# A fused graph-attention kernel: step 0's small transfers on another queue, and the last span's sums ended in two halves

## The chip, the cores and the metric

The kernel runs on one core of one Trainium2 chip. The metric is the device time of one execution in microseconds (us), and a comparison uses the median of several runs. The core has five engines that run their own instruction lists in order and meet through semaphores: TensorE (PE, matrix products, with its weight loads shown as PEld), VectorE (DVE), ScalarE (ACT), GpSimd (POOL) and SyncE (SP). Transfers between memory and the core's buffers are issued from the list of an engine, here SP's or ACT's, and run on 16 DMA engines. SP does nothing but issue transfers.

## What is computed

Two layers work on x (2708 x 256) and adj (2708 x 2708). Cut to what matters:

```python
# layer 0: two steps of row-normalised adjacency and of sparse attention
R = (adj + I) / row_sums
for n in range(2):
    A  = top_p(softmax((Xa @ W1.T @ W2.T) @ (Xa @ W3.T).T), 0.9)   # rows re-normalised
    Xf = R @ Xf
    Xa = A @ Xa
    Z += Xf @ U1[n].T + Xa @ U2[n].T
x = layernorm(x + layernorm(x + Z))
# layer 1: graph attention with 4 heads of 64
Wh = einsum('nd,hdo->nho', x, W)
e  = leaky_relu(s_i[:, None] + s_j[None, :], 0.2)     # s_i, s_j: Wh times the halves of a
h  = softmax(e where adj or diagonal, over j) applied to Wh
x  = layernorm(x + h.reshape(n, 256))
```

## The kernel before

The 2708 rows are 22 tiles: 16 of 128 rows and 6 of 110 (`rows`, `off`). Most work is float32.

**Layer 0, step 0** (about 95 to 470 us of the trace). For each tile t, `step` multiplies its attention weights with all 22 tiles of values. The weights e have to be turned first: `turned` makes transposes on PE (`tr`, L266) and a copy on ACT (`eT`, L271), one group of up to four tiles ahead of the products (`att`, L284). Between groups, `slot` advances other work by one piece: searches for the top-p threshold of later tiles (DVE, ACT, POOL), and what comes after a finished tile. That last is `after_attention0`: it turns the tile's result, projects it for the next step's scores after every second tile (`project`) and multiplies it with the second pair of U matrices (`terms2`). Both of the latter end in a small transfer:

- `project` copies half of the query rows into the partition range `there` of qT (L766) and then moves them to the other half of the partitions with a transfer (L767, 55 to 64 KB). `begun` is empty before step 0 starts and set from then on, so the seven transfers of the first projection are SP's and the twelve of step 0 are ACT's.
- `terms2` copies a product into the buffer cs (L1257; two of these buffers rotate), a second one into ba (L1258), and stores cs to memory as c (L1259, 110 to 128 KB, one for each of the 22 tiles). The stores are read back when layer 0 is finished, after 500 us.

Beside this runs `mixes`: for each of 11 pairs of tiles SP loads four blocks of adj (L677), POOL adds and subtracts them, and SP stores the sums (L683) for a fast matrix product of layer 0's other half, `walks`, which loads them back (L689) from the end of step 0 on.

**Layer 1.** Targets are worked on in three `spans` of 8, 8 and 6 tiles (1024, 1024 and 660 columns). For each span a loop takes the 22 source tiles in pairs. `weights` makes the four heads' unnormalised weights pt on DVE (L1602), into three sets of buffers; `values` multiplies them with the source's values (L1614), `denominators` with its column sums (L1624), each head or half head in a quarter of PE's columns. Products are summed in six PSUM banks `acc`, for two head pairs and the denominators, each in two column pieces `cuts`, 512 and the rest (148 in the last span). After the last pair the banks are copied to `val` (L1717) and `den` (L1725), the first piece by ACT, the second by DVE.

`settle` then finishes one target tile, in pieces that a loop advances in turn: three transposes on PE (L1532, L1533), a reciprocal on DVE (L1535), the scaled result `res`, the add of the residual xe on POOL (L1551), and in the last span the layer norm: statistics on DVE (L1558 to L1560), a power and a product on POOL (L1561, L1562), the normalised tile o on ACT (L1564; two buffers o rotate) and its store by SP (L1565). In the last span res is made on ACT, a head at a time (L1546), for even tiles, and on DVE, in one operation (L1541), for odd ones. Tiles of the first two spans are settled beside the next span's products; those of the last span after all products, from six homes in PSUM.

In layer 0 (from `query_weights` on) and layer 1 the order of PE, DVE, ACT and POOL is the order in which the program issues their instructions.

Of the kernel before, what the change touches and what calls it, by code (L numbers as in the profile page):

```python
# [12 lines left out]
ALU = mybir.AluOpType  # L13
# [7 lines left out]
CHUNK = 512  # L21
# [24 lines left out]
def kernel(  # L46
# [16 lines left out]
    nc = tc.nc  # L63
    N, D = x.shape
    DA = w1T.shape[1]
    STEPS = u1T.shape[0]
    H, _, FO = gat_w.shape
# [3 lines left out]
    rows = [P] * 16 + [110] * 6  # L71
# [31 lines left out]
    xe = const.tile([P, NT, D + 2], F32, name="xe")  # L103
# [448 lines left out]
    def fast_layer0(ep, adjp):  # L552
# [196 lines left out]
        def project(s, c0, w, pj, xT, copy_q, copy_k):  # L749

            for lo, hi, h in ((c0, min(c0 + w, HN), 0), (max(c0, HN), c0 + w, 1)):
                if lo >= hi:
                    continue
                here, there = slice(h * DA, (h + 1) * DA), slice((1 - h) * DA, (2 - h) * DA)
                at = slice(lo - c0, hi - c0)
                for c in range(DC):  # L760
                    nc.tensor.matmul(
                        pj[:, at], wkqk[:, c, h : h + 2].rearrange("p h e -> p (h e)"),
                        xT[:, c, at], start=(c == 0), stop=(c == DC - 1),
                    )
                copy_k(kT[s][here, lo - h * HN : hi - h * HN], pj[here, at])
                copy_q(qT[there, lo:hi], pj[there, at])  # L766
                (nc.scalar if begun else nc.sync).dma_start(qT[here, lo:hi], qT[there, lo:hi])  # L767

        def turn(src, m, tp, copy, xT=None):

# [476 lines left out]
        def terms2(t, xT):  # L1247

            m = rows[t]
            cy = free_bank().rearrange("p a b -> p (a b)")  # L1250
            for c in range(DC):
                nc.tensor.matmul(
                    cy[:m], xT[:, c, :m], u_sb[:, 1, c].rearrange("p s e -> p (s e)"),
                    start=(c == 0), stop=(c == DC - 1),
                )
            cs = rowp.tile([P, D], F32, name="cs")
            nc.scalar.copy(cs[:m], cy[:m, 0:D])  # L1257
            nc.scalar.copy(ba[:m, t, :], cy[:m, D : 2 * D])  # L1258
            nc.scalar.dma_start(c2[t][:m], cs[:m])  # L1259

        def finish(t, xw, ca, cb):

# [133 lines left out]
        with tc.manual_schedule(engines=engines):  # L1396
            query_weights()
            ahead = turn_x(groups[0])
            for n in range(len(groups)):
                c0, w = ahead  # L1400
# [95 lines left out]
    def layer1(ep, adjp, r=None, verdict=None, early=()):  # L1496
# [19 lines left out]
        def bank(k, c):  # L1516
            return ps_v[k][c].tile([P, CHUNK], F32, name=f"acc{k}_{c}")
# [6 lines left out]
        def aux():  # L1524
            return ps_u.tile([P, H, P], F32, name="aux")

        def settle(g, t, val, den, u, last):

            m = rows[t]
            cols = slice(off[t] - off[spans[g][0]], off[t + 1] - off[spans[g][0]])  # L1530
            for q in range(2):
                nc.tensor.transpose(u[:m, q, :], val[:, q, cols], ident)  # L1532
            nc.tensor.transpose(u[:m, 2, :], den[:, cols], ident)  # L1533
            rden = small.tile([P, H], F32, name="rden")
            nc.vector.reciprocal(  # L1535
                rden[:m], u[:m, 2, :].rearrange("p (h o) -> p h o", h=H)[:, :, 0]
            )
            res = pp.tile([P, H, FO], F32, name="res", bufs=5)
            sums = u[:m, 0:2, :].rearrange("p q (h o) -> p (q h) o", h=2)
            if last and t % 2:  # L1540
                nc.vector.tensor_tensor(  # L1541
                    res[:m], sums, rden[:m].unsqueeze(2).to_broadcast([m, H, FO]), op=ALU.mult
                )
            else:
                for h in range(H):
                    nc.scalar.activation(  # L1546
                        res[:m, h, :], sums[:, h, :], AF.Copy, scale=rden[:m, h : h + 1]
                    )
            yield
            flat = res[:m].rearrange("p h o -> p (h o)")  # L1550
            nc.gpsimd.tensor_add(flat, flat, xe[:m, t, 0:D])  # L1551
            yield
            o = pp.tile([P, D], F32, name="o")[:m]
            if last:
                st = small.tile([P, 6], F32, name="ln_st")[:m]
                mv = small.tile([P, 2], F32, name="ln_mv")[:m]
                ve, rs, nb = (small.tile([P, 1], F32, name=f"ln_{k}")[:m] for k in ("ve", "rs", "nb"))
                nc.vector.bn_stats(st, flat)  # L1558
                nc.vector.bn_aggr(mv, st)
                nc.vector.tensor_scalar(ve, mv[:, 1:2], LN_EPS, None, op0=ALU.add)  # L1560
                nc.gpsimd.tensor_tensor(rs, ve, minus_half[:m], op=ALU.pow)  # L1561
                nc.gpsimd.tensor_scalar(nb, mv[:, 0:1], rs, -1.0, op0=ALU.mult, op1=ALU.mult)  # L1562
                yield
                nc.scalar.activation(o, flat, AF.Identity, scale=rs, bias=nb)  # L1564
                nc.sync.dma_start(out[off[t] : off[t + 1], :], o)  # L1565
                return
            yield from layernorm_beside(o, flat, m)
            yield
            nc.scalar.dma_start(out[off[t] : off[t + 1], :], o)
# [10 lines left out]
        cuts = []  # L1580
        for span in spans:
            gw = off[span[-1] + 1] - off[span[0]]
            cuts.append([(c, min(CHUNK, gw - c)) for c in range(0, gw, CHUNK)])
        targets, masks, probs, acc = {0: r}, {}, {}, {}

        def mask(n):
# [17 lines left out]
                        bar, op0=ALU.max, op1=ALU.mult,  # L1604
                    )

        def values(n, heads):
            g, at, j = order[n]
            k, at = rows[j], dict(start=(at == 0), stop=(at == NT - 1), skip_group_check=True)
            for c, (c0, w) in enumerate(cuts[g]):  # L1610
                for h in heads:
                    for o in range(0, FO, SIDE):
                        to = h % 2 * FO + o
                        nc.tensor.matmul(  # L1614
                            acc[h // 2][c][to : to + SIDE, :w],
                            v[j][:k, h, o : o + SIDE], probs[n][h][:k, c0 : c0 + w], **at,
                        )

        def denominators(n):
            g, at, j = order[n]  # L1620
            k, at = rows[j], dict(start=(at == 0), stop=(at == NT - 1), skip_group_check=True)
            for c, (c0, w) in enumerate(cuts[g]):
                for h in range(H):
                    nc.tensor.matmul(  # L1624
                        acc[2][c][h * SIDE : (h + 1) * SIDE, :w],
                        sb[:k, j, h : h + 1].to_broadcast([k, SIDE]),
                        probs[n][h][:k, c0 : c0 + w], **at,
                    )
            del probs[n]

        def prepared(t):

# [64 lines left out]
        for n in range(0, len(order), 2):  # L1697
            g, i, j = order[n]
            beside(g, i)
            weights(n + 2)  # L1700
            mask(n + 3)
            if i == 0:
                acc = [
                    [bank(k, c) for c in range(len(cuts[g]))]
                    for k in range(3)
                ]
            last = i + 2 == NT
            if last:
                val = pp.tile([P, 2, GW], F32, name="val", bufs=1)
                den = pp.tile([P, GW], F32, name="den", bufs=1)  # L1710
            for u in (n, n + 1):
                for k in range(2):
                    values(u, (2 * k, 2 * k + 1))
                    if last and u > n:
                        for c, (c0, w) in enumerate(cuts[g]):
                            copy = nc.scalar.copy if c == 0 else nc.vector.tensor_copy
                            copy(val[:, k, c0 : c0 + w], acc[k][c][:, :w])  # L1717
            if not last:
                beside(g, i + 1)
            for u in (n, n + 1):  # L1720
                denominators(u)
            if last:
                for c, (c0, w) in enumerate(cuts[g]):
                    copy = nc.scalar.copy if c == 0 else nc.vector.tensor_copy
                    copy(den[:, c0 : c0 + w], acc[2][c][:, :w])  # L1725
                assert not rest
                rest = [(g, t, val, den) for t in spans[g]]
            weights(n + 3)
            mask(n + 4)
        assert not late  # L1730

        homes = [bank(k, c) for k in range(2) for c in range(2)]
        while rest or running:
            new = []
            if rest:
                u = homes.pop(0).rearrange("p (h m) -> p h m", h=H) if homes else aux()
                new = [settle(*rest.pop(0), u, True)]
                next(new[0])
            running = [p for p in running[::-1] if next(p, running) is not running][::-1] + new
        l1.close()  # L1740

    with ExitStack() as both:
# [58 lines left out]
```

## Time and profile before

| | us |
|---|---|
| median of 3 runs | 1546.16 |
| lowest and highest of them | 1543.17, 1548.04 |
| the profiled execution's own time | 1544.92 |
| its span in the trace | 1543.1 |
| mean granted clock of TensorE | 0.994 |

The page's slices (40 of 38.6 us each) show where the engines work, in tenths:

```profile
PE   7999999999999899999999999999999999999995
DVE  3698999888614887888889898998895998999995
ACT  3444445444426655665655666666653444456474
POOL 0057576654013422323354544544443320035133
DMA  6188988885027745544474565555446355334331
```

Step 0 covers slices 3 to 12. DMA is its busiest part: the mixing loads and stores run there, and end well before the step does. Layer 1 starts near 1200 us. The last slice is where PE has run out of products.

In the lists of groups and waits, `x` gives a count, `out<-in` the buffers written and read, and `<-` in brackets or after the wait what ended the idle time. ACTq and SPq are transfers issued from these engines' lists. ACT's largest waits of step 0's stretch:

```profile
ACT e L795 <- PE lg L791: 50.1, 20, 2.9
ACT cs L1257 <- PE walk L1252: 47.3, 19, 2.9
ACT eT L271 <- PE tr L266: 40.9, 34, 1.8
...
ACT eT L271 <- DMA scr<-in_adjT_dram: 11.8, 4, 5.7
ACT eT L271 <- ACT qT L766: 4.4, 8, 0.6
ACT eT L271 <- DMA D<-blk: 3.1, 2, 1.7
```

The columns are us in total, times, and the longest. The last three lines are idle time before an eT copy that was ended neither by PE nor by a search.

### The profile page before, as it was taken

The page shows a single profiled execution, that of the slowest core. Times are in us where ns is not written, and L with a number is a line of the kernel's source. Part 1 is how long each engine was busy: PE and PEld are TensorE (multiplying, and loading weights), DVE is VectorE, ACT ScalarE, POOL GpSimd, SP SyncE. Part 2 cuts the span into 40 slices and gives each one's busy share as a digit, 9 for nine tenths or more (in the row PEclk, how much of TensorE's full clock was granted, in tenths as well). Part 3 has the DMA queues.
Part 4 walks back from the last instruction along what each step waited for, and adds up shares of the span by engine and source line. Part 5 has one row for each costly group of instructions (what it writes and reads, how often), then busy time and mean ns, then how long its engine had stood idle before and what let it go on. Part 6 is the DMA issues. An engine that isn't in the chain of part 4 may idle for free. (4 is left out here: it accounts for less than half of the span.)

```text
span 1543.1 us, 29894 instructions
## 1 busy us (share of the span) xinstructions
PE 1494.1 (97%) x10537; PEld 1066.1 (69%) x10537; DVE 1275.3 (83%) x3741; ACT 807.7 (52%) x1494; POOL 590.6 (38%) x962
## 2 busy tenths in 40 slices
PE   7999999999999899999999999999999999999995
PEld 4476767677679888998888888888898223433343
DVE  3698999888614887888889898998895998999995
ACT  3444445444426655665655666666653444456474
POOL 0057576654013422323354544544443320035133
PEclk9999999999999999999999999999999999999998
DMA  6188988885027745544474565555446355334331
GB/s 167 63 251 280 283 273 255 267 263 168 8 77 223 228 160 169 166 151 147 146 210 126 176 193 160 187 168 176 130 146 185 104 179 170 97 107 131 87 111 46
DMA packets 214489, 255.98 MB, mean 166 GB/s; under 512 B 42145, under 2 KB 180541, under 8 KB 214329
## 3 DMA queue, kind: packets, MB, share of 16 engines
q1 hardware_dynamic: 201632, 243.15, 51.7%
q10 hardware_dynamic: 12697, 10.82, 2.3%
q8 instruction: 85, 1.39, 0.4%
q14 instruction: 75, 0.61, 0.1%
HBM read 190.10 MB, written 62.44 MB: 164 GB/s over the span
## 5 line engine op out<-in xcount | busy, mean ns | idle before, releaser
L816 ACT ACTIVATE junk<-e,minus,rth 128x2708 bf16<-128x2708 f32 (+1 forms) x88 | 232.9, 2646 | 52.5 <-POOL rth L848 51.7
L271 ACT COPY eT<-tr 128x512 f32<-128x512 f32 (+5 forms) x264 | 141.4, 536 | 213.4 <-PE tr L266 189.0
L284 PE MATMUL att<-xm,eT 128*128 128x256 f32 (+3 forms) x968 | 232.0, 381 | 0.4 <-ACT xa L1325 0.4
L284 PE MATMUL att<-ba,eT 128*128 128x256 f32 (+3 forms) x968 | 231.6, 380 | 0.0
L1614 PE MATMUL acc<-pt,v 128*32 128x512 f32 (+3 forms) x2112 | 221.0, 543 | 1.9 <-DVE pt L1602 1.2
L1602 DVE SCALAR_TENSOR_TENSOR pt<-e,tj,blk 128x1024 f32<-128x1024 f32 (+3 forms) x176 | 186.6, 1126 | 9.4 <-ACT xw L1265 6.5
L284 PEld LDWEIGHTS att<-xm,eT 128*128 128x128 f32 (+3 forms) x968 | 170.5, 187 | 22.4 <-ACT xa L1325 0.8
L284 PEld LDWEIGHTS att<-ba,eT 128*128 128x128 f32 (+3 forms) x968 | 170.1, 187 | 22.2 <-ACT eT L271 0.8
L795 ACT ACTIVATE e<-lg 128x1024 f32<-128x1024 f32 (+1 forms) x132 | 121.1, 922 | 106.6 <-PE lg L791 105.7
L1109 PE MATMUL walk<-xe,blk 128*128 128x128 f32 (+3 forms) x1386 | 172.9, 275 | 1.2 <-ACT xw L1123 0.7
L1109 PEld LDWEIGHTS walk<-xe,blk 128*128 128x128 f32 (+1 forms) x1386 | 164.4, 187 | 11.4 <-issue 7.4
L1614 PEld LDWEIGHTS acc<-pt,v 128*32 128x32 f32 (+1 forms) x2112 | 73.2, 110 | 132.3 <-issue 99.7
L266 PE MATMUL tr<-ident,e 128*128 128x128 f32 (+3 forms) x968 | 148.7, 272 | 12.1 <-ACT eT L271 11.9
L266 PEld LDWEIGHTS tr<-ident,e 128*128 128x128 f32 (+3 forms) x968 | 111.6, 139 | 55.9 <-issue 25.7
L1109 PE MATMUL walk<-xm,blk 128*128 128x128 f32 (+3 forms) x1034 | 130.4, 276 | 4.5 <-DVE u_sb L1119 2.7
L1109 PEld LDWEIGHTS walk<-xm,blk 128*128 128x128 f32 (+3 forms) x1034 | 123.3, 187 | 12.8 <-issue 6.1
L896 DVE MAX8 cand<-e 128x8 f32<-128x170 f32 (+1 forms) x352 | 88.0, 322 | 46.3 <-ACT e L795 46.3
L1624 PE MATMUL acc<-pt,sb 128*32 128x512 f32 (+3 forms) x1056 | 114.8, 542 | 0.0
L1602 DVE SCALAR_TENSOR_TENSOR pt<-r,tj,blk 128x1024 f32<-128x1024 f32 (+1 forms) x88 | 109.9, 1314 | 1.2 <-PE acc L1624 0.4
L247 ACT ACTIVATE blk<-blk 128x1024 f32<-128x1024 f32 (+3 forms) x66 | 63.2, 960 | 81.6 <-DMA blk<-in_adjT_dram 80.1
L896 DVE MAX8 cand<-scr 128x8 f32<-128x97 f32 (+1 forms) x616 | 102.9, 244 | 0.0
L802 POOL TENSOR_TENSOR fact<-zp 128x1 f32<-128x1 f32 (+1 forms) x44 | 30.0, 681 | 170.2 <-ACT e L795 170.2
(280 smaller groups left out, 2453.9 us busy)
## 6 DMA issues: line engine op xcount, KB each, us to landing
blk<-in_adjT_dram SPq DMA_DIRECT2D x68, 512.0 KB
blk<-S SPq DMA_DIRECT2D x48, 512.0 KB
blk<-D SPq DMA_DIRECT2D x24, 512.0 KB
blk<-in_adjT_dram SPq DMA_DIRECT2D x26, 440.0 KB
D<-blk SPq DMA_DIRECT2D x16, 512.0 KB
S<-scr SPq DMA_DIRECT2D x16, 512.0 KB
S<-blk SPq DMA_DIRECT2D x16, 512.0 KB
xm<-S SPq DMA_DIRECT2D x16, 512.0 KB
```

The lines of the kernel that those rows point to most:

```text
L247: nc.scalar.activation(bar, bar, AF.Sign)
L266: nc.tensor.transpose(tr[: rows[t], q, :m], e[:m, off[t] : off[t + 1]], ident[:m, :m])
L271: copy(eT[:k, : len(grp), :m], tr[:k, : len(grp), :m])
L284: nc.tensor.matmul(acc, eT[: rows[t], q, :m], value(t), start=(t == 0), stop=(t == NT - 1),)
L795: nc.scalar.activation(halves[:m, :, c0 : c0 + w], lg[:m, :, :w], AF.Exp, accum_out=zp[:m, n : n + 1],)
L802: nc.gpsimd.tensor_add(z, zp[:m, 0:1], zp[:m, 1:2])
L816: nc.scalar.activation(junk[:m], e[:m], func, scale=rth, bias=minus1[:m], accum_out=acc)
L896: nc.vector.max(cand[:, n, :], src[:m, n * size : min(N, (n + 1) * size)])
L1109: nc.tensor.matmul(ac, blk[:k, j, :], MOVING[name](j, k, w), start=start and j == 0, stop=j == PAIRS - 1, skip_group_check=True,)
L1602: nc.vector.scalar_tensor_tensor(pt[:k, :gw], targets[g][h // 2][:k, h % 2, :gw], tj[:k, j, h : h + 1], bar, op0=ALU.max, op1=ALU.mult,)
L1614: nc.tensor.matmul(acc[h // 2][c][to : to + SIDE, :w], v[j][:k, h, o : o + SIDE], probs[n][h][:k, c0 : c0 + w], **at,)
L1624: nc.tensor.matmul(acc[2][c][h * SIDE : (h + 1) * SIDE, :w], sb[:k, j, h : h + 1].to_broadcast([k, SIDE]), probs[n][h][:k, c0 : c0 + w], **at,
```

## The change

Four edits. The transfers of `project` and of `terms2` are always issued by SP. In the last span the column pieces are two halves of 330 columns, three tiles each. The last pair of sources of the last span goes through a new function, `closing`: it takes the first half's products of both sources, with their denominators, then the second half's of the first source, then starts to settle the three tiles of the first half, then takes the second half's products of the last source and settles the other three. Copies of the values are made by ACT for heads 0 and 1 and by DVE for heads 2 and 3, those of the denominators by ACT. And in `settle`, odd tiles of the last span get their residual in the same DVE operations that scale, one for each head, so that POOL's add falls away for them.

```diff
-                (nc.scalar if begun else nc.sync).dma_start(qT[here, lo:hi], qT[there, lo:hi])
+                nc.sync.dma_start(qT[here, lo:hi], qT[there, lo:hi])
...
-            nc.scalar.dma_start(c2[t][:m], cs[:m])
+            nc.sync.dma_start(c2[t][:m], cs[:m])
...
+            flat = res[:m].rearrange("p h o -> p (h o)")
             if last and t % 2:
-                nc.vector.tensor_tensor(
-                    res[:m], sums, rden[:m].unsqueeze(2).to_broadcast([m, H, FO]), op=ALU.mult
-                )
+                for h in range(H):
+                    nc.vector.scalar_tensor_tensor(
+                        res[:m, h, :], sums[:, h, :], rden[:m, h : h + 1],
+                        xe[:m, t, h * FO : (h + 1) * FO], op0=ALU.mult, op1=ALU.add,
+                    )
...
             yield
-            flat = res[:m].rearrange("p h o -> p (h o)")
-            nc.gpsimd.tensor_add(flat, flat, xe[:m, t, 0:D])
-            yield
+            if not (last and t % 2):
+                nc.gpsimd.tensor_add(flat, flat, xe[:m, t, 0:D])
+                yield
...
-            cuts.append([(c, min(CHUNK, gw - c)) for c in range(0, gw, CHUNK)])
+            part = CHUNK if span is not spans[-1] else len(span) // 2 * rows[span[0]]
+            cuts.append([(c, min(part, gw - c)) for c in range(0, gw, part)])
...
+        def begin(t, val, den, home):
+            new = settle(len(spans) - 1, t, val, den, home, True)
+            next(new)
+            step_on()
+            running.append(new)
+
+        def step_on():
+            running[:] = [p for p in running[::-1] if next(p, running) is not running][::-1]
+
+        def closing(n, val, den):
+
+            per = len(spans[-1]) // 2
+            early_ones, late_ones = spans[-1][:per], spans[-1][per:]
+            for c, (c0, w) in enumerate(cuts[-1]):
+                these = slice(c, c + 1)
+                for u in (n, n + 1):
+                    if c and u > n:
+                        for k, t in enumerate(early_ones):
+                            begin(t, val, den, bank(k, 0).rearrange("p (h m) -> p h m", h=H))
+                    for k, copy in enumerate((nc.scalar.copy, nc.vector.tensor_copy)):
+                        values(u, (2 * k, 2 * k + 1), these)
+                        if u > n:
+                            copy(val[:, k, c0 : c0 + w], acc[k][c][:, :w])
+                    denominators(u, these)
+                nc.scalar.copy(den[:, c0 : c0 + w], acc[2][c][:, :w])
+            for k, t in enumerate(late_ones):
+                home = aux() if k < 2 else bank(0, 1).rearrange("p (h m) -> p h m", h=H)
+                begin(t, val, den, home)
+            while running:
+                step_on()
...
+            if last and g == len(spans) - 1:
+                closing(n, val, den)
+                break
...
-        homes = [bank(k, c) for k in range(2) for c in range(2)]
-        while rest or running:
-            new = []
-            if rest:
-                u = homes.pop(0).rearrange("p (h m) -> p h m", h=H) if homes else aux()
-                new = [settle(*rest.pop(0), u, True)]
-                next(new[0])
-            running = [p for p in running[::-1] if next(p, running) is not running][::-1] + new
```

`values` and `denominators` take a third argument, the pieces to work on.

More of the change, by code (lines that the diff above doesn't have):

```diff
@@ L1605, in weights, with values @@
                     )
-        def values(n, heads):
+        def values(n, heads, these=None):
             g, at, j = order[n]
             k, at = rows[j], dict(start=(at == 0), stop=(at == NT - 1), skip_group_check=True)
-            for c, (c0, w) in enumerate(cuts[g]):
+            for c, (c0, w) in list(enumerate(cuts[g]))[these or slice(None)]:
                 for h in heads:
@@ L1617, in values, with denominators @@
                         )
-        def denominators(n):
+        def denominators(n, these=None):
             g, at, j = order[n]
             k, at = rows[j], dict(start=(at == 0), stop=(at == NT - 1), skip_group_check=True)
-            for c, (c0, w) in enumerate(cuts[g]):
+            for c, (c0, w) in list(enumerate(cuts[g]))[these or slice(None)]:
                 for h in range(H):
@@ L1628, in denominators @@
                     )
-            del probs[n]
+        def begin(t, val, den, home):
[25 more added lines that the diff above has]
+                step_on()
         def prepared(t):
@@ L1721, in layer1 @@
                 denominators(u)
+                del probs[u]
             if last:
```

## The prediction

> **What bounds the kernel now.** I read the page's busy line first, then the waits of TensorE, then the two places the change touches: layer 0's step 0 (95 to 470 us) and the tail after 1509 us.
>
> ```profile
> PE 1494.1 (97%) x10537; PEld 1066.1 (69%) x10537; DVE 1275.3 (83%) x3741; ACT 807.7 (52%) x1494; POOL 590.6 (38%) x962
> ```
>
> TensorE (PE) is busy 1494.1 of 1543.1 us, so a gain is a PE gap closed or something after PE's last product. For step 0, PE's own waits between 95 and 470 us, then ScalarE (ACT) in order of time around the longest of them and around a later one:
>
> ```profile
> PE tr L266 <- ACT eT L271: 5.5, 4, 3.3
> PE lg L774 <- ACT xa L1325: 0.6, 1, 0.6
> PE walk L761 <- ACT qT L766: 0.5, 1, 0.5
> ...
> 112.09 0.37 ACT L766 COPY qT<-walk 64x256 f32<-64x256 f32 x1
> 117.64 0.50 ACTq L767 DMA_DIRECT2D qT<-qT  x1
> 118.18 0.59 ACT L271 COPY eT<-tr 128x512 f32<-128x512 f32 x1 [5.72 <-DMA scr<-in_adjT_dram]
> ...
> 275.24 0.38 ACT L1258 COPY ba<-walk 128x256 f32<-128x256 f32 x1
> 277.53 0.33 ACTq L1259 DMA_DIRECT2D c<-cs  x1
> 277.90 0.59 ACT L271 COPY eT<-tr 128x512 f32<-128x512 f32 x1 [2.28 <-DMA scr<-in_adjT_dram]
> ```
>
> ACT finished qT's copy at 112.46 but issued the transfer after it only at 117.64; the copy of eT that PE needed stood behind it, and ACT's idle time ended with a landing of scr, a block that the transfer has nothing to do with. In the program's list of waits every transfer waits for an earlier one that used the same of eight completion semaphores, so a small store issued by ACT can wait for a 512 KB load that SyncE (SP) issued. PE's four gaps before L266 are 3.25 us (to 118.82), 0.35 (172.31), 0.49 (227.72) and 1.44 (278.54), together 5.53, and each follows such an issue on ACT.
>
> The first gap costs more than itself. Busy time by stretch (us of PE, PEld, DVE, ACT, POOL; clock; DMA share; GB/s):
>
> ```profile
> 115.20:118.60 3.40, 0.36 (x1) 0.00 (x0) 3.19 (x6) 0.42 (x1) 3.40 (x4) 1.00 0.97 319
> 118.60:122.00 3.40, 3.18 (x10) 2.73 (x11) 3.37 (x5) 1.30 (x4) 3.40 (x4) 0.50 0.99 382
> 122.00:125.40 3.40, 3.40 (x18) 2.50 (x18) 3.40 (x3) 0.37 (x1) 3.40 (x2) 1.00 0.80 304
> ```
>
> After an idle stretch PE runs 3.4 us at half clock: 1.7 us of work lost. In the tail, the chain of waits (start, us, what) shows PE's last products, and the timeline (start, us, engine, line) a result on DVE, the first adds on POOL and the last output tile:
>
> ```profile
> 1521.89 1.99 PE acc L1624 x18
> 1523.89 0.02 issue
> 1523.91 0.59 ACT den L1725
> ...
> 1525.52 0.42 DVE L1541 TENSOR_TENSOR res<-acc,rden 110x256 f32<-110x256 f32 x1
> ...
> 1526.13 1.31 POOL L1551 TENSOR_TENSOR res<-res,xe 110x256 f32<-110x256 f32 x2 [9.01 <-ACT res L1546]
> ...
> 1535.94 0.60 ACT L1564 ACTIVATE o<-res,ln_nb,ln_rs 110x256 f32<-110x256 f32 x1 [0.56 <-DMA out_dram<-o]
> ```
>
> Products end at 1523.89, the last o at 1536.54, the span at 1543.1. In the 12.65 us between, GpSimd (POOL) sets the pace: each of six tiles takes an add (0.64 to 0.72), a power (0.55) and a product (0.27) there, about 1.5 us.
>
> [...]
>
> **The change, part by part.**
>
> *A. Step 0's transfers go to SP.* Twelve qT transfers (L767) and 22 c stores (L1259) leave ACT's queue. Of PE's time: 5.53 us of gaps go, and 3.4 x 0.5 = 1.7 us of slow clock with the first. Sum 7.2. The issue time that ACT sheds (12 x 0.47 + 22 x 0.33 = 12.9 us) is worth nothing more, because ACT is 42% busy there (156.2 of 375 us) and other eT copies come in time. What is late next: VectorE's (DVE) searches, 93.1 of 100 us busy between 200 and 300. They are ahead, though: DVE's last reciprocal of step 0 ends at 420.29, and the last tile, whose result ACT copies at 449.71, starts some 18 us before that, near 431, so 7 us fits.
>
> On SP every issue counts. Thirty-four more take 12.9 us, and each waits for ACT's copy. I set each new place in SP's list against the times of before: at 24 of the 34, the SP transfer just behind it was issued 0.5 to 8.5 us after ACT's copy was done, at three the copy is 0.03 to 0.35 us later, and seven fall where SP idles until 449.28 anyway. Queued behind them are the mixing loads and stores (L677, L683). Those end at 366.2, and four block loads at 369; the next SP load then waits for PE until 449.28. That is the cover, 80 us, against 24 moved issues (about 9.5 us) before it. Only two stand after 449, with ACT's copies done at 455.26 and 460.06 and SP's next issues at 456.35 and 460.53: up to 0.5 us for a walk load, where PE has gaps on loads at 503.5 and 507.6 us. I take 0, bound 0 to 1. The stores land later by 5 to 10 us; their two cs buffers turn over every 15 us per tile, c is read after 500 us, qT's other half by the next step's rows. No wait there.
>
> *B. The tail.* I laid out the last pair of sources and the settling by hand, in the new order of each engine's list, with durations of before's rows; the same layout of the old order ends at 1536.43 (traced: 1536.54). One pair's 96 product records take 4.58 + 2.22 = 6.80 us. A half (330 columns) of one source is thus 1.70, of it 0.57 for denominators. A 330-column width costs the same per column as 512 and 148, so the rest of the span is priced at 0.
> - PE: start 1516.7; first source's first half to 1518.4. The last source's weights come from DVE at 1518.09, 1518.90, 1519.72, 1520.54 as before (they wait for a buffer that PE frees at 1516.7). So PE waits 0.5, works 0.57, waits 1.1, works 1.14: 1521.7. First source's second half: 1523.4. Nine transposes at 0.11: 1524.4. Last source's second half: 1526.1, 2.2 us later than before.
> - Early tiles: ACT's result of the first 1524.2 to 1525.1, POOL's add to 1525.9, its mean and variance on DVE to 1527.1. Behind this in DVE's list stands the second half's val copy: 1527.1 to 1527.55, while PE had that product at 1525.6.
> - Late tiles: transposes from 1527.6; DVE's four-operation results and statistics end 1530.0 (tile 19), 1530.8, 1532.7, 1533.5; POOL's last power and product 1533.7 to 1534.6; last o 1534.65 to 1535.24.
>
> Against 1536.43 that is 1.2 us earlier. Three adds (2.0 us) leave POOL, but DVE gains three sets of four. Not in the trace: a 64-column scalar_tensor_tensor from PSUM. Below, a quarter of the 256-column row at L1541 (0.425/4), so 0.12; above, the 56-column L955 at 0.28 to 0.335. [...] I take 0.20. Twelve of them: the gain runs from 1.9 (0.12) through 1.2 to a loss of 0.6 (0.35). The 6.6 us after the last o stay.
>
> Sum: 7.2 + 1.2 = 8.4. The profiled execution took 1544.92, which gives 1536.5; the median of the three is 1546.16, which gives 1537.8. I say 1537.
>
> **Rivals.**
> 1. *Half of A stays.* DVE at 93% becomes step 0's pace, or the half-clock stretch moves: a gap of 2.7 us at 807.7 is followed by one, a gap of 2.4 at 1189.6 is not[...]. Then only the 3.3 of the long gap and B's 1.2 come: 1541.7. For: DVE's share. Against: its lead at the end of the step.
> 2. *The tail gives B back.* DVE operations cost 0.35, the copy of val is later: B is +0.6, total 6.6 less, 1539.5. For: DVE has the most new work, and PE's products end later.
> 3. *SP holds the mixing (slower).* A store waiting for ACT holds all mixing transfers behind it, POOL waits for loads, ACT and PE come later in turn. Place: SP between 96 and 369 us; price: the hold of each of 24 moved issues; it decides once these average 80/24 = 3.3 us. At 4 us, 16 us late: 1546.2 - 8.4 + 16 = 1554. For: DMA is 88 to 90% busy from 100 to 300 us. Against: ACT's copies are ready ahead of SP nearly everywhere.
> 4. *It doesn't do what it says*: the gaps reappear on ACT for another transfer; B alone, 1545. Against: no transfer is left on ACT in step 0.
>
> **How the numbers follow.** Forecast 0.58, rival 1 0.17, rival 2 0.10, rival 3 0.09, rival 4 0.06. A measurement here tells 0.3% (4.6 us; faster is below 1541.5). Faster: 0.55 of the forecast, 0.09 of rival 2, 0.05 of rival 1, 0.69. Slower: rival 3, 0.09. The rest, 0.22, within. Range: low end 1537.8 less 1.7 (a second half-clock stretch gone), 0.7 (B at its best) and 2.9 (the lowest run against the median): 1532.5. High end past rival 1 with half of the runs' spread: 1544. That leaves out rivals 3 and 4.
>
> **What would show it.** Right: no waits of ACT's eT copy on DMA between 95 and 470 us, PE's wait there on eT under 1 us, no half clock near 118, step 0 ending near 442; SP's mixing done by 385. In the tail: products ending about 2.2 us later against the start of the last pair, DVE's second val copy 1.5 us after its product, last o about 18.6 us after that start (19.8 before). Wrong: new PE gaps in step 0 with releaser DVE or DMA, SP still issuing mixing stores after 430, or four DVE results per tile taking over 1.2 us.

## The result, and the profile after

| | before | after |
|---|---|---|
| median, us (5 runs of each) | 1544.79 | 1534.79 |
| lowest and highest, us | 1541.94, 1548.04 | 1533.26, 1537.31 |
| span of the profiled execution, us | 1543.1 | 1532.7 |

The ratio is 0.993, with a 95% interval of 0.9916 to 0.9944. The kernel is faster by 10.0 us; the prediction said 1537 us.

I read the profile after in the order in which the one before was read. First the page's busy line:

```profile
PE 1492.8 (97%) x10537; PEld 1064.6 (69%) x10537; DVE 1277.1 (83%) x3749; ACT 804.9 (53%) x1495; POOL 594.5 (39%) x959
```

PE's work is the same (10537 instructions) and takes 1.3 us less; the rest of the gain must be time in which PE idled. Then PE's waits between 95 and 470 us (line, what it waited for, us in total, times, longest), and ACT in order of time (start, us, what) where it had stood for 5.2 us:

```profile
PE lg L774 <- ACT xa L1325: 0.6, 1, 0.6
PE walk L761 <- ACT qT L766: 0.5, 1, 0.5
PE att L284 <- ACT xa L1325: 0.3, 2, 0.2
```

```profile
112.10 0.37 ACT L766 COPY qT<-walk 64x256 f32<-64x256 f32 x1
112.49 0.58 ACT L271 COPY eT<-tr 128x512 f32<-128x512 f32 x1
```

The first line of the old list, 5.5 us for eT, is gone. The copy of eT starts at 112.49, directly behind qT's copy, where it had started at 118.18. The end of step 0 is read here as the start of PE's transposes at L774 that follow the step's last att product: 450.24 us before, 441.91 after. The windows from 95 us to it in each kernel (length; busy PE, PEld, DVE, ACT, POOL; clock; DMA share; GB/s), before first, and then, in after, the same stretch of time that had run at half clock before:

```profile
95.00:450.24 355.24, 348.12 (x1740) 252.30 (x1739) 290.78 (x853) 150.91 (x336) 186.37 (x206) 1.00 0.68 211
```

```profile
95.00:441.91 346.91, 345.49 (x1741) 251.51 (x1739) 291.71 (x853) 148.32 (x336) 192.51 (x206) 1.00 0.70 216
118.60:122.00 3.40, 3.40 (x18) 1.76 (x17) 3.40 (x2) 1.16 (x3) 3.40 (x4) 1.00 1.00 398
```

Step 0 is 8.33 us shorter. PE's idle time in it fell from 7.12 (355.24 - 348.12) to 1.42 us, which is 5.70; its busy time fell by 2.63, of which 1.61 is the half-clock stretch, as worked out further down (the clock column now has 1.00 there).

In the tail, the chain of waits of after (start, us, what), and PE's last products and first transposes of the late tiles in its timeline:

```profile
1516.18 0.86 DVE res L1543 x4
1517.05 0.09 DVE rden L1535
1517.13 0.38 DVE ln_st L1561
1517.54 0.19 DVE ln_mv L1562
1517.76 0.15 DVE ln_ve L1563
1517.91 0.35 DVE ln_st L1561
...
1518.65 0.42 DVE val L1656
...
1526.08 0.60 ACT o L1567
```

```profile
1517.25 0.74 PE L1628 MATMUL acc<-pt,sb 110*32 110x330 f32 x8
1518.47 0.32 PE L1532 MATMUL aux<-ident,val 128*110 128x128 f32 x1 [0.48 <-ACT val L1656]
1519.12 0.32 PE L1532 MATMUL aux<-ident,val 128*110 128x128 f32 x1 [0.32 <-DVE val L1656]
```

The chain now runs through DVE, where before POOL set the pace. DVE works without a break from the first fused result to the second half's val copy, which waits behind the statistics of two early tiles; PE's transposes for the late tiles wait for it.

To compare tails of traces that are shifted against each other I use one mark: the start of DVE's last operation on the diagonal (L251), shortly before the last sources' weights, at 1516.81 us before and 1508.31 after. From there the last o ends after 19.73 us before and 18.37 after, 1.36 less. PE's products end after 7.31 and 9.68. The whole difference of the two spans, -10.45 us, is then:

| stretch | difference, us |
|---|---|
| step 0, to the first transposes of xa (L774) | -8.33 |
| from there to the start of the tail | -0.17 |
| tail, from the mark to the end of the last o | -1.36 |
| after the last o | -0.59 |

I put the two differences in rows 2 and 4 down to no edit: the time after the last o lies between 5.62 and 7.09 us over all traces of the study, and the largest parts of row 2 are a gap of PE at 1182 us that is shorter (1.29 against 2.44) and one at 1280 that is longer (1.81 against 0.49). Over all traces the first lies between 1.20 and 2.66 us and the second between 0.45 and 2.13, and after_again, the same kernel as after, has 1.49 and 0.50.

### The profile page after: what moved, and what is told of

Its sections match the earlier page's. It is cut to its first block, busy times and chain, and to the rows that moved or that the text cites. A ratio compares the mean times of both kernels' runs of the same rounds, so it can differ in the third digit from the quotient of the medians.

```text
span 1532.7 us, 29967 instructions
## 1 busy us (share of the span) xinstructions
PE 1492.8 (97%) x10537; PEld 1064.6 (69%) x10537; DVE 1277.1 (83%) x3749; ACT 804.9 (53%) x1495; POOL 594.5 (39%) x959
## 5 line engine op out<-in xcount | busy, mean ns | idle before, releaser
L1109 PE MATMUL walk<-xe,blk 128*128 128x128 f32 (+3 forms) x1386 | 172.9, 275 | 1.2 <-ACT xw L1123 0.7
L1109 PEld LDWEIGHTS walk<-xe,blk 128*128 128x128 f32 (+1 forms) x1386 | 164.4, 187 | 11.4 <-issue 7.4
L266 PE MATMUL tr<-ident,e 128*128 128x128 f32 (+3 forms) x968 | 147.5, 271 | 4.8 <-ACT eT L271 4.8
L266 PEld LDWEIGHTS tr<-ident,e 128*128 128x128 f32 (+3 forms) x968 | 111.3, 139 | 47.1 <-issue 26.7
L1109 PE MATMUL walk<-xm,blk 128*128 128x128 f32 (+3 forms) x1034 | 131.3, 277 | 5.4 <-DVE u_sb L1119 2.9
L1109 PEld LDWEIGHTS walk<-xm,blk 128*128 128x128 f32 (+3 forms) x1034 | 124.2, 188 | 14.0 <-issue 6.1
L914 DVE MAX8 top<-work 128x8 f32<-128x128 f32 (+3 forms) x242 | 82.3, 340 | 8.3
```

The source lines that it names most:

```text
L266: nc.tensor.transpose(tr[: rows[t], q, :m], e[:m, off[t] : off[t + 1]], ident[:m, :m])
L914: nc.vector.max(top[:, k : k + 8], work if k else flat)
L1109: nc.tensor.matmul(ac, blk[:k, j, :], MOVING[name](j, k, w), start=start and j == 0, stop=j == PAIRS - 1, skip_group_check=True,)
```

## The experiments

Ten runs, each timed in 5 rounds beside the kernel before on the same chip. The table has what the readings below rest on; times in us, the tail and the products' end counted from the mark above.

| kernel | ratio (95%) | step 0 ends | PE gaps over 0.15 us in step 0 | products end | last o ends |
|---|---|---|---|---|---|
| before | | 450.24 | 6.98 | 7.31 | 19.73 |
| after | 0.993 (0.9916, 0.9944) | 441.91 | 1.42 | 9.68 | 18.37 |
| a_alone | 0.9928 (0.9914, 0.9941) | 442.23 | 1.42 | 7.30 | 19.73 |
| b_alone | 1.0001 (0.9991, 1.0012) | 450.15 | 6.69 | 9.68 | 18.37 |
| q_only | 1.0018 (1.0005, 1.003) | 451.93 | 8.85 | 7.31 | 19.74 |
| c_only | 0.9979 (0.9969, 0.9989) | 448.62 | 6.17 | 7.31 | 19.75 |
| filler | 0.9934 (0.9919, 0.9949) | 441.67 | 1.45 | 9.68 | 18.37 |
| no_fusion | 0.9938 (0.9923, 0.9953) | 440.97 | 1.42 | 9.68 | 19.65 |
| fusion_alone | 0.9921 (0.9908, 0.9934) | 441.21 | 1.42 | 7.31 | 18.26 |
| reorder | 0.9927 (0.9912, 0.9942) | 440.71 | 1.42 | 8.01 | 17.06 |

**Each part by itself.** a_alone is the kernel before with the two moved transfers; b_alone is the changed kernel with these two lines as they were.

```diff
 a_alone, against before:
-                (nc.scalar if begun else nc.sync).dma_start(qT[here, lo:hi], qT[there, lo:hi])
+                nc.sync.dma_start(qT[here, lo:hi], qT[there, lo:hi])
...
-            nc.scalar.dma_start(c2[t][:m], cs[:m])
+            nc.sync.dma_start(c2[t][:m], cs[:m])
```

> The kernel before with both kinds of step 0's transfers on SyncE's queue and the tail as it was. Theory (the wait of ACT's issue on another transfer's completion held the eT copies): step 0's end, read as the start of TensorE's transposes at L774 that follow its last att product (450.24 us before, 441.91 after), comes at 442 to 443; no ACT wait of an eT copy on a DMA there; time 8 to 9 us below before, ratio about 0.9945. Rival (the two edits work only together, the step's gain being given back before the end): step 0 ends early but the time falls by less than 5 us. The tail, from the start of the diagonal's operation on DVE before the last four weights to the end of the last o, stays at 19.7 us.

> The changed kernel with step 0's transfers back on ScalarE's queue, so the new tail alone. Theory: step 0 ends at 450 as before, with the gap before 118.8 and the half clock after it; the tail takes 18.4 us (19.7 before), so the time falls by 1 to 2 us, ratio 0.999. Rival (the gain belongs to the tail and step 0's was a shift that would have vanished): the time falls by 5 us or more. Another rival (the halves cost more than they bring without A): slower by up to 1 us.

The parts are independent: step 0 ends with a_alone where it does with both (442.23 and 441.91), and b_alone's tail is that of both (18.37). The moved transfers alone give the whole measured gain, 0.72%. That is about 11 us, more than the 8 to 9 expected; step 0 ends 8.0 us earlier in the trace, and where the rest lies isn't shown (the trace is that of the slowest of six executions). The tail's 1.36 us are 0.09% of the time, too small for an interval of 0.1% to each side: b_alone's time can't be told from before's.

**Which of the transfers.** q_only moves only qT's transfers to SP, c_only only the c stores.

```diff
 q_only, against a_alone:
-            nc.sync.dma_start(c2[t][:m], cs[:m])
+            nc.scalar.dma_start(c2[t][:m], cs[:m])
 c_only, against a_alone:
-                nc.sync.dma_start(qT[here, lo:hi], qT[there, lo:hi])
+                (nc.scalar if begun else nc.sync).dma_start(qT[here, lo:hi], qT[there, lo:hi])
```

> The kernel before with qT's twelve transfers alone on SyncE's queue; the 22 c stores stay on ScalarE's. Theory that each stall belongs to the transfer it was seen at: the gap at 118.8 (3.25 us) and the half clock (1.7 us) go, the three gaps behind c stores (2.3 us) stay: step 0 ends at 445, time 5 us lower. Rival (the stalls go to whichever ACT transfer meets a big load's completion, so those that remain meet others): new gaps behind c stores, step 0 ends at 446 to 450.

> The kernel before with the 22 c stores alone on SyncE's queue; qT's twelve transfers stay on ScalarE's. Theory that each stall belongs to its transfer: gaps at 172, 228 and 279 (2.3 us) go, the long one at 118.8 with the half clock stays: step 0 ends at 447.5 to 448, time 2 to 3 us lower. Rival (stalls go to whichever transfer meets a big load): other gaps behind qT transfers, or the long one gone, so the step's end anywhere from 442 to 450.

The longest gap of before, 3.25 us, stood behind a transfer of qT. With all of these on SP, q_only has one of 3.59 us, one eT copy later, as PE's waits and then ACT in order of time show:

```profile
PE tr L266 <- ACT eT L271: 7.4, 4, 3.6
```

```profile
116.01 0.38 ACT L1258 COPY ba<-walk 128x256 f32<-128x256 f32 x1
120.44 0.34 ACTq L1259 DMA_DIRECT2D c<-cs  x1
120.83 0.59 ACT L271 COPY eT<-tr 110x512 f32<-110x512 f32 x1 [4.44 <-DMA D<-blk]
```

The first c store now takes the stall: its data were ready at 116.39, ACT issued it at 120.44, and what ended ACT's idle time was the landing of D, one of SP's mixing stores. Four such waits cost PE 7.4 us where before's cost 5.5, and q_only is slower than before by 0.18% (0.05% to 0.3%). In c_only the long gap stays where it was, and a second, of 1.16 us at 225.59, stands behind another qT transfer, where before had 0.14:

```profile
112.14 0.37 ACT L766 COPY qT<-walk 64x256 f32<-64x256 f32 x1
118.01 0.49 ACTq L767 DMA_DIRECT2D qT<-qT  x1
118.54 0.59 ACT L271 COPY eT<-tr 128x512 f32<-128x512 f32 x1 [6.04 <-DMA scr<-in_adjT_dram]
```

So a stall belongs neither to qT nor to c alone. The semaphores in the traces' instruction records show why. Transfers signal their landings on eight semaphores, numbered 100 to 107, which ACT's and SP's transfers share, and an issue can have to wait until an earlier transfer on the same number has landed. In before, ACT's issue at 117.64 waits for number 100, last used by SP's load of scr (issued 111.08, landed 117.56), and the c store at 120.34 for number 104, last used by SP's store of D (landed 120.26). q_only has that second wait too (landed 120.36, issued 120.44). It was there in before, hidden behind qT's. The prediction had such a wait at every transfer; the record shows it at eight of ACT's 34 issues of before, five of 22 in q_only and four of 12 in c_only. The earlier transfer is SP's each time, and all but one of the 17 issues come 0.08 us after its landing (before the one, at 187.14 of before, it had landed already). PE's waits for eT in these three traces, four, four and two, all stand behind such issues.

Half the edit brings nothing or about three tenths (0.21%) of the gain; all of it comes when ACT issues no transfer in step 0.

**Is it the wait, or the issue's own time?** filler is the changed kernel with some of ACT's time given back as work: copies that nothing reads, three where each of qT's transfers had been issued and two for each c store.

```diff
+                if begun:
+                    for _ in range(3):
+                        nc.scalar.copy(filler, ident[:, 0:64].unsqueeze(1).to_broadcast([P, 3, 64]))
...
+            for _ in range(2):
+                nc.scalar.copy(filler, ident[:, 0:64].unsqueeze(1).to_broadcast([P, 3, 64]))
```

> The changed kernel with ACT work put where the issues were: three copies of 192 columns after each of step 0's twelve qT transfers' place, two after each of the 22 c stores' place, some 0.2 us each, 16 us together, more than the 12.9 us that issuing took. Theory (the wait cost, the issue time did not): step 0 still ends at 442 to 443, time within 1 us of the changed kernel, ratio to before about 0.994. Rival (ACT's time in these places was the cost): step 0 ends 3 to 8 us later and the time rises accordingly.

The window of step 0, to be set against that of after above:

```profile
95.00:441.67 346.67, 345.22 (x1741) 251.40 (x1739) 293.87 (x852) 172.21 (x411) 193.39 (x206) 1.00 0.70 216
```

ACT has 75 instructions and 23.9 us more (172.21 - 148.32), nearly twice the 12.9 us of issues that it shed, and step 0 ends at the same time with PE as busy. The issue time was worth nothing; the waits were all of it.

**The two edits of the tail.** no_fusion keeps the halves and takes back the fused residual; fusion_alone fuses the residual and keeps the old order of the products. Both have step 0's transfers on SP.

```diff
 no_fusion, against after:
-                for h in range(H):
-                    nc.vector.scalar_tensor_tensor(
-                        res[:m, h, :], sums[:, h, :], rden[:m, h : h + 1],
-                        xe[:m, t, h * FO : (h + 1) * FO], op0=ALU.mult, op1=ALU.add,
-                    )
+                nc.vector.tensor_tensor(
+                    res[:m], sums, rden[:m].unsqueeze(2).to_broadcast([m, H, FO]), op=ALU.mult
+                )
...
-            if not (last and t % 2):
-                nc.gpsimd.tensor_add(flat, flat, xe[:m, t, 0:D])
-                yield
+            nc.gpsimd.tensor_add(flat, flat, xe[:m, t, 0:D])
+            yield
```

> The changed kernel with odd tiles of the last span as before: one scaling operation on DVE and the residual's add on POOL; the closing in two halves stays. By the layout POOL again takes three adds of 0.65 to 0.72 us, DVE gets three times 0.45 us less. Theory (DVE sets the new tail, so the fused operations cost about what the adds saved): the tail stays within 0.5 us of 18.4 us. Rival (POOL still sets it and the fusion carries the gain): the tail grows by 1 to 2 us, to 19.4 to 20.4 us.

> The kernel before with step 0's transfers on SyncE's queue and the fused residual, but with all products before all settling and pieces of 512 and 148 columns. Theory (POOL's 1.5 us per tile set the old tail, and three adds of 0.64 to 0.72 leave it): the tail takes 18.0 to 18.7 us instead of 19.7. Rival (the halves carry the gain): the tail stays at 19.3 to 20 us.

Without the fusion the tail is 19.65 us, nearly before's 19.73. I had expected it near 18.4, with DVE setting the end; POOL's timeline in no_fusion shows why it isn't:

```profile
1519.44 0.55 POOL L1561 TENSOR_TENSOR ln_rs<-ln_ve,minus_half 110x1 f32<-110x1 f32 x1 [0.71 <-DVE ln_ve L1560]
...
1520.31 0.64 POOL L1551 TENSOR_TENSOR res<-res,xe 110x256 f32<-110x256 f32 x1
1520.91 0.55 POOL L1561 TENSOR_TENSOR ln_rs<-ln_ve,minus_half 110x1 f32<-110x1 f32 x1
1521.55 0.26 POOL L1562 TENSOR_SCALAR ln_nb<-ln_mv,ln_rs 110x1 f32<-110x1 f32 x1
1521.78 0.72 POOL L1551 TENSOR_TENSOR res<-res,xe 110x256 f32<-110x256 f32 x1
```

From there on add, power and product follow each other without a wait, one tile each 1.47 us (1521.78 - 1520.31), as before: POOL is the bound again. Its first add starts 8.47 us after the mark, 0.85 earlier than before's (9.32), but the wait in the first line takes 0.71 of that back: the statistics of the second early tile stand on DVE behind val's copy and a late tile's result. fusion_alone has the full gain, 19.73 - 18.26 = 1.47 us. The halves, then, bring 0.08 us without the fusion and cost 0.11 with it (18.37 against 18.26).

**Can the halves be made to pay?** In after, PE waits for the last source's weights inside the first half (they end on DVE at 1512.05, and the chain goes on with PE's products at 1512.09), and the val copy of the second half stands behind two tiles' statistics on DVE. reorder gives PE both halves of the first source before it needs the last one's weights, and issues the copies ahead of the early tiles.

```diff
+            for c in range(2):
+                values(n, range(H), slice(c, c + 1))
+                denominators(n, slice(c, c + 1))
             for c, (c0, w) in enumerate(cuts[-1]):
                 these = slice(c, c + 1)
-                for u in (n, n + 1):
...
+                for k, copy in enumerate((nc.scalar.copy, nc.vector.tensor_copy)):
+                    values(n + 1, (2 * k, 2 * k + 1), these)
+                    copy(val[:, k, c0 : c0 + w], acc[k][c][:, :w])
+                if c:
+                    for k, t in enumerate(early_ones):
+                        begin(t, val, den, bank(k, 0).rearrange("p (h m) -> p h m", h=H))
+                denominators(n + 1, these)
```

> The changed kernel with another order in the closing: both halves of the first source's products come first, then the last source's first half, then its second half's values, then the early tiles' transposes, then its second half's denominators; copies of the values stand ahead of the early tiles' statistics. Theory (the two waits of TensorE for the last weights, 0.5 and 1.1 us, and the val copy held on DVE cost the tail): products end 1.7 us sooner after the last pair's start, the tail takes 17.0 to 17.5 us instead of 18.4. Rival (DVE's or POOL's work per tile sets the tail whatever the start): 18.0 to 18.6 us.

The chain of waits of reorder:

```profile
1511.29 1.11 PE acc L1618 x14
...
1513.53 0.86 DVE res L1543 x4
...
1515.44 0.33 ACT den L1659
...
1515.81 0.33 PE aux L1533
...
1522.67 0.60 ACT o L1567
```

The val copy is off the chain; what the late tiles wait for is now ACT's den copy, which stands behind ACT's results of an early tile. The tail is 17.06 us, 1.31 less than after's, and the products end 8.01 us after the mark instead of 9.68. Which of the two moves brings how much was not measured apart.

Is that faster in time? after_again and reorder_again are the same two kernels, measured together.

> The changed kernel once more, beside the re-ordered one on the same chip. Its ratio to the kernel before was 0.993 (0.9916 to 0.9944). Theory that the differences of about 0.1% between the kernels that keep step 0's change are noise (half-clock stretches that come or not): the ratio comes out anywhere from 0.9915 to 0.994 and its interval overlaps that of the re-ordered kernel. Rival, that the tail's 1.3 us (0.08%) can be seen in the time: above the re-ordered kernel's interval.

> The re-ordered tail once more. First measured at 0.9927 (0.9912 to 0.9942). Theory of noise: anywhere from 0.991 to 0.994, the interval overlapping that of the changed kernel. Rival: 1.3 us below the changed kernel's median, that is 0.08% lower, with the intervals apart.

after_again took 1534.49 us (ratio 0.9935, 0.9923 to 0.9947) and reorder_again 1531.87 (0.992, 0.9907 to 0.9933). The re-ordered median is the lower one both times, by 1.8 and 2.6 us, and both its traces have the shorter tail (17.06 and 17.05 against 18.37 twice). But the intervals overlap: reorder is faster than before for certain, and faster than after by 1.3 us in the trace alone; the times don't decide it.

## Why the prediction was right

**Step 0** (said: 5.53 of gaps, 1.7 of half clock, 7.2 in sum, ending near 442). It ended at 441.91. Both terms are confirmed in kind, and lining up PE's transposes (L266) of the two traces gives their sizes. After's lead grows by 3.41 us at the long gap (118.82 before, 115.41 after), by 1.61 in the half-clock stretch behind it (122.59 and 117.57), and by 0.55, 0.36, 0.70 and 1.65 at the gaps before 172.31, 224.86, 227.72 and 278.54: in sum 8.28 of the 8.33. The half clock thus cost 1.61 where 1.7 was said, and the gaps 6.67 where 5.53 was. Each costs about 0.2 us more than its listed idle time, and the prediction's list lacks the one at 224.86, of 0.14 us, which stands behind a qT transfer too. ACT's issue time at nothing is confirmed by filler. DVE's lead sufficed, so rival 1 has no place: its work in the window is the same (290.78 and 291.71) and PE has no new wait for it. Rival 4, the gaps that reappear on ACT for another transfer, is false of the whole change and true of half of it, as q_only shows.

**SP** (said: its cover is 80 us, the price 0 to 1, the mixing done by 385). SP in order of time, after:

```profile
373.79 0.30 SPq L683 DMA_DIRECT2D S<-scr  x1
...
391.83 14.62 SPq L1259 DMA_DIRECT2D c<-cs  x2
...
440.94 0.97 SPq L677 DMA_DIRECT2D xm<-in_adjT_dram  x2
```

The last mixing store is issued at 373.79, 7.6 us later than before (366.2), of the size of the 9.5 us that 24 issues were said to take. SP's waits for ACT's copies up to there add up to 3.3 us, where rival 3 needed 3.3 for each issue, so it fails: of 80 us of cover, a tenth was used. Six more loads follow by 377.42. From then to 440.94, where the list goes on with loads, stores of c stand for up to 14 us with nothing behind them that anyone waits for. The price behind step 0 was 0: the stretch up to the last of PE's gaps there (450.24 to 523.85 before, 441.91 to 515.06 after) is 0.46 us shorter, not longer.

**The tail** (said: 1.2 us less, last o 18.6 after the start against 19.8; products 2.2 later; DVE's val copy 1.5 late; fused operations 0.20 each). Measured: 1.36 less, 18.37 against 19.73; products 2.37 later; the copy at 1518.65, when the record of PE's product ends at 1517.44, 1.2 late; four fused operations in 0.86 us, one issued each 0.19 to 0.20. So the layout by hand held, rival 2 with it fell, and the 0.28 to 0.335 of the nearest row would have been too high a price: 0.28 is the length of one, but they overlap. The two rows that the prediction names bound the 0.20 and don't give it; no trace ahead of the result showed it. (The prediction's lower price, 0.425/4, is 0.11 and not 0.12; this touches its best case alone.) The equal price of a column at widths of 330 and of 512 and 148, which was an estimate, held: from one pair of sources in the last span to the next PE took 7.28 us before (1459.24 to 1466.52) and 7.29 after (1450.71 to 1458.00). What the prediction did not separate is which edit brings it. It gave the halves and the fusion one number, and the experiments give the fusion all of it. So the number was near and half of its account was not right: the earlier start of three tiles is worth 0.08 us alone and costs 0.11 beside the fusion.

**The sum.** 8.4 was predicted; the trace has 10.45 and the medians differ by 10.0. Of the trace's 2.05 us more, 1.13 lie in step 0, 0.16 in the tail, and 0.76 in the stretches that were priced at nothing. The last part is chance.

## What to carry to other kernels

When an engine that a critical chain runs through also issues transfers, look at its timeline for the time between a transfer's data being ready and its issue, and at what ended that wait: if it is an unrelated landing, try the stage with no transfer issued by that engine at all, since here moving some of them left or uncovered the waits of the others. Before splitting work to start its second part earlier, ask which engine is back to back behind it; here the gain came from taking three adds off that engine, and the split paid only once two waits inside it were gone. A part worth 0.1% can be read in a trace and not in times that vary by 0.3%.

## What the runs showed of the hardware

Half-clock stretches come and go with no change at their place. A gap of 2.5 to 3.1 us of PE near 801 us (about 810 where step 0 is longer) is in all twelve traces. No stretch at half clock goes with it in five of them (gaps of 2.54 to 2.91 us), one of 3.41 us in five (2.71 to 3.12), and one twice as long in two (2.93 and 3.12).

In the twelve traces every stretch of one clock but the last, which the end of the trace cuts, is a whole number of 3.413 us long; before has 31 such lengths at full clock, one at half, 202 at full, one at half and 210 at full. Below, a window is one such length, counted from a change of the clock. With these windows laid over PE's records, those at full clock before PE's last instruction fall in two groups: the 15 in which PE is busy for 1.50 us or less are each followed by half clock, and none with 1.55 us or more is. Of the windows at half clock, the three with up to 2.71 us busy are followed by another, those from 2.84 us on are not. So of gaps of about the same length some had half clock behind them and some not, as more or less of a gap lay in one window; that this is the cause was not shown. after_again and reorder_again, either side of the bound, and a_alone, which has two at half clock (columns as above; each line is one window):

```profile
799.07:802.49 3.42, 1.50 (x13) 1.50 (x14) 3.08 (x17) 2.88 (x3) 0.19 (x1) 1.00 0.62 208
802.49:805.90 3.41, 3.41 (x13) 2.96 (x13) 3.27 (x14) 1.99 (x2) 0.00 (x0) 0.50 0.00 0
...
799.23:802.64 3.41, 1.55 (x13) 1.55 (x14) 3.06 (x17) 2.89 (x3) 0.16 (x1) 1.00 0.61 205
802.64:806.05 3.41, 3.41 (x26) 3.20 (x25) 3.28 (x13) 2.65 (x2) 0.00 (x0) 1.00 0.00 0
...
802.06:805.47 3.41, 2.71 (x12) 2.71 (x13) 3.06 (x17) 1.92 (x3) 0.00 (x0) 0.50 0.30 112
805.47:808.89 3.42, 3.42 (x13) 2.98 (x12) 3.42 (x13) 1.88 (x2) 0.00 (x0) 0.50 0.00 0
```

The bounds are read from traces that differ by chance, not set on purpose, and the ends of PE's products in a trace are modelled. After the products one window breaks them (no_fusion, 1.69 us busy from 1516.37, then half clock). In before, the window ahead of the stretch at 118.6 us has 0.36 us of work. At half clock PE started a product of 128 columns (L1109) every 0.213 us (after, from 801.47), at full clock every 0.112 (before, from 814.94). From these I estimate that a window at half clock costs about half of its busy time, 1.7 us at most (the one at 118.6 us cost 1.61), so two executions of one kernel can differ by that, more than the whole tail edit was worth (1.36 us). after_again's six executions have mean granted clocks from 0.993 to 0.997, with the lowest in the slowest of them.
